# Grouped query attention on one core: one query product for all heads, spread by transfers within SBUF, and values of 32 columns

## The chip, the cores and the metric

The kernel runs on one core of one Trainium2 chip. Its five engines run their own instruction queues and meet through semaphores: TensorE (PE) multiplies matrices into PSUM, VectorE (DVE) and ScalarE (ACT) read PSUM and SBUF, GpSimd (POOL) does the indirect transfers and some elementwise work, and SyncE (SP) issues most transfers. The metric is the device time of one execution in microseconds, the median of several runs, without the profiler.

## The reference

The program is a two-layer block over x of 16 sequences, 256 tokens each, 128 features, all in float32. Layer 0 is half a mixture of experts, grouped query attention, half the same mixture again. Layer 1 is half a zone network, latent attention, half the zone network again. The part that is changed is layer 0's attention:

```
q = x @ Wq + bq                      # 16 heads of 8 columns
k = x @ Wk + bk                      # 4 key heads of 8 columns
v = x @ Wv + bv                      # 4 value heads of 8 columns
q = q.reshape(B, N, 4, 4, 8)         # key head g, query head j of the group, d
scores = einsum('bghnd,bhsd->bghns', q, k)
attn = softmax(scores / sqrt(8))
out  = einsum('bghns,bhsd->bghnd', attn, v) @ Wo + bo
```

Here x has been layer-normalised. Each key head g serves the four query heads 4g to 4g+3.

## The kernel before, in words

Tokens are split into eight blocks of 512 (two sequences each, `TB = 512`, `NB = 2`). The blocks stay in SBUF as `xs[0..7]` through the whole program. The stages follow one another: experts (`moe_first`), attention (`gqa`), experts (`moe_second`), zones, latent attention (`mla`), zones.

The attention keeps key head g in partition rows 32g to 32g+31, of which eight hold the head's columns, so that four products with 32 rows of contraction can stand in four row quarters of the PE array. The matrices are laid out for this on the host (`_layout`, helper `columns`): `w_q0` is four matrices of 128x128, one for each j, mostly zeros; `w_k0` and `w_v0` are 128x128 with the same gaps.

For each block, `gqa_rest` (L889) gives a list of small steps, `todo`: `head` (transposes the normalised block to `xnT`, L894; POOL adds the output bias to x, L896), `keys` (one product, L905, and an ACT evacuation, L906), `queries(j)` for four j (a product 128x512, L910, and an evacuation with scale and bias, by DVE for even j, L913, by ACT for odd j, L915) and `values` (four products 128x128, L922, and a DVE evacuation with bias, L925). The tiles `kT`, `qT` and `v` have three buffers each. The row after the eight columns of each head carries a one in the keys and in the values, and in the queries the negated largest score.

`gqa` (L1072) runs over sequences, n = 0 to 19, in four overlapping steps: the sequence `new` gets its scores and their maxima (`score` L937, the DVE reduction L976); `last` sends its maxima into the spare rows of `qT` (`send_largest`: PE transposes L1011, a DVE copy L1013, four transfers from SP, L1016); `old` gets the transposed scores with the maxima in them (`again` L949) and ACT's exponential (L980); `older` is multiplied with the values (`weigh` L1026), divided by its sums (`over_sums` L1043 to L1048) and finally turned and projected (`turned` L1058, `project` L1068). Each n has eight units, k = 0 to 7. One unit is eight products `score` or `again`, two reductions and two exponentials (`units` L959). After each unit PE gets a few `pieces`, among them one step of the next block's `todo`: in the block's first sequence (b = 0) after units 5, 6 and 7, in its second (b = 1) after units 0, 5, 6 and 7 (L1112). In n = 0 and 1 there is no `old`, and `wide_units` (L982, reductions L992) is used; n = 14 and 15 have no next block, so no `todo` steps.

Between these steps stand pieces of other work (`ahead`, from `beside_attention` L836): the shared expert of the first mixture (L634, L642, L643, L652) in n = 0 and later, and the routing of the second mixture from n = 8 on. At the start of each block, `gqa_pre(t + 1)` adds the experts' results to the next block on DVE (L788, eight operations) and normalises it.

The scores and exponents have three PSUM banks each, and all other products share two, the tag `pb` (L63). A scheduler orders the instructions of each engine when the program is built; each engine then runs its own list in that order.

POOL's list at the turn from experts to attention is: the two bias additions L896, then the gathers `y<-moe_y` (L772, eight for each block) that fetch the experts' results. The first of these waits until the last experts' tile has been written to DRAM (L745).

Of the kernel before, what the change touches and what calls it, by code (L numbers as in the profile page):

```python
# [12 lines left out]
F32 = mybir.dt.float32  # L13
I32 = mybir.dt.int32
U32 = mybir.dt.uint32
AF = mybir.ActivationFunctionType
ALU = mybir.AluOpType
# [3 lines left out]
P = 128  # L21
D = 128
SEQ = 256
TB = 512
NB = TB // SEQ
NTT = TB // P
NST = SEQ // P
# [10 lines left out]
H0, G0, J0, HD0 = 16, 4, 4, 8  # L38
SCALE0 = HD0 ** 0.5
# [11 lines left out]
def macaron_kernel(ctx: ExitStack, tc: tile.TileContext, a: dict, out: bass.AP):  # L51
# [3 lines left out]
    nc = tc.nc  # L55
# [4 lines left out]
    cpool = ctx.enter_context(tc.tile_pool(name="const", bufs=1))  # L60
# [4 lines left out]
    psum, stage = {}, {}  # L65
# [5 lines left out]
    def pb(shape):  # L71
        return psb.tile(shape, F32, tag="pb", name="pb")


    def load(name, shape=None, start=0):
        src = a[name]
        t = cpool.tile(list(shape or src.shape), F32, tag=name, name=name)
        nc.sync.dma_start(t[start : start + src.shape[0]], src)
        return t

    def load_rows(name):
        src = a[name]
        t = cpool.tile([P, src.shape[0]], F32, tag=name, name=name)
        nc.sync.dma_start(t, src.partition_broadcast(P))
        return t
# [54 lines left out]
    tile_no = counting("tile_no", NSLOT, 1)  # L140
    w_q0, w_k0, w_v0, w_o0 = load("w_q0"), load("w_k0"), load("w_v0"), load("w_o0")
    b_q0, b_k0 = load("b_q0"), load("b_k0")
    b_qs = cpool.tile([P, J0], F32, tag="b_qs", name="b_qs")
    nc.gpsimd.tensor_scalar(b_qs, b_q0, 1.0 / SCALE0, None, ALU.mult)
    b_v0, b_o0 = load_rows("b_v0"), load_rows("b_o0")
    w_r1, b_r1, w_r2, b_r2 = load("w_r1"), load("b_r1"), load("w_r2"), load_rows("b_r2")
# [143 lines left out]
    def turn_block(xn):  # L290
        xnT = pre.tile([P, TB], F32, name="xnT")
        transpose4(xn, xnT)
        return xnT
# [53 lines left out]
    for c in range(2):  # L347
        s = cpool.tile([P, 4, AHEAD + NPT, E0], F32, tag=f"sums{c}", name=f"sums{c}")
# [537 lines left out]
    def gqa_pre(t):  # L886
        return gqa_rest(t, normalised(t))

    def gqa_rest(t, xn):  # L889

        q = dict(t=t)

        def head():
            q["xnT"] = turn_block(xn)  # L894
            xt = xs[t]
            nc.gpsimd.tensor_tensor(  # L896
                xt, xt, b_o0.unsqueeze(1).to_broadcast([P, NTT, D]), ALU.add
            )

        def keys():  # L900
            pool = stage["pool"]
            q["kt"] = pool.tile([P, TB], F32, name="kT", bufs=3)
            q["qa"] = pool.tile([P, J0, TB], F32, name="qT", bufs=3)
            pk = pb([P, TB])
            nc.tensor.matmul(pk, w_k0, q["xnT"], start=True, stop=True)  # L905
            nc.scalar.activation(q["kt"], pk, AF.Identity, bias=b_k0)  # L906

        def queries(j):
            pq = pb([P, TB])
            nc.tensor.matmul(pq, w_q0[:, j, :], q["xnT"], start=True, stop=True)  # L910
            dst, bias = q["qa"][:, j, :], b_qs[:, j : j + 1]
            if j % 2 == 0:
                nc.vector.tensor_scalar(dst, pq, 1.0 / SCALE0, bias, ALU.mult, ALU.add)  # L913
            else:
                nc.scalar.activation(dst, pq, AF.Identity, bias=bias, scale=1.0 / SCALE0)  # L915

        def values():

            q["v"] = stage["pool"].tile([P, NTT, P], F32, name="v", bufs=3)
            pv = pb([P, NTT, P])  # L920
            for i in range(NTT):
                nc.tensor.matmul(  # L922
                    pv[:, i, :], q["xnT"][:, ts(i, P)], w_v0, start=True, stop=True
                )
            nc.vector.tensor_tensor(  # L925
                q["v"], pv, b_v0.unsqueeze(1).to_broadcast([P, NTT, P]), ALU.add
            )

        q["todo"] = [head, keys] + [partial(queries, j) for j in range(J0)] + [values]
        return q  # L930

# [84 lines left out]
    def weigh(q, half, s):  # L1018

        b, v, pT = q["b"], q["v"], q["pT", half]  # L1020
        if s == 0:
            q["po"] = pb([P, 2, SEQ])
            if half == 0:
                q["ov"] = stage["pool"].tile([P, J0, SEQ], F32, name="ov", bufs=2)
        for g in range(G0):
            nc.tensor.matmul(  # L1026
                q["po"][ts(g, 32)],
                v[:, b * NST + s, ts(g, 32)],
                pT[:, s, g, :],
                start=(s == 0),  # L1030
                stop=(s == NST - 1),
            )
        if s == NST - 1:
            copy = nc.vector.tensor_copy if half == 0 else nc.scalar.copy
            copy(q["ov"][:, ts(half, 2), :], q["po"])
# [36 lines left out]
    def gqa(block, after):  # L1072

        seqs = []
        rest = None

        def at(n):
            return seqs[n] if 0 <= n < len(seqs) else None

        ahead = after()  # L1080
        for f in block["todo"]:
            f()
        for n in range(2 * NBLK + 4):
            t, b = divmod(n, NB)
            if t < NBLK:
                if b == 0:
                    if rest is not None:
                        block = rest
                    rest = None
                    if t + 1 < NBLK:  # L1090
                        with tc.issue_after(reduced["last"].ins) if n else ExitStack():
                            rest = gqa_pre(t + 1)
                seqs.append(dict(block, b=b))
            elif n == 2 * NBLK:
                rest = None

            new, last, old, older, oldest = at(n), at(n - 1), at(n - 2), at(n - 3), at(n - 4)
            if n >= 2 * NBLK:
                new = None
            pieces = [[] for _ in range(8)]  # L1100
            if last is not None and n <= 2 * NBLK:
                pieces[0].append(partial(send_largest, last))
            if oldest is not None:
                pieces[0].append(partial(turned, oldest))
                pieces[2].append(partial(project, oldest))
            if older is not None:
                for k in range(4):
                    pieces[1 + k].append(partial(weigh, older, k // 2, k % 2))
                pieces[6].append(partial(over_sums, older, 0))
                pieces[7].append(partial(over_sums, older, 1))  # L1110
            if rest is not None and t < NBLK:
                for k in (5, 6, 7) if b == 0 else (0, 5, 6, 7):  # L1112
                    pieces[k].append(rest["todo"].pop(0))
            for k in range(8):
                half, s, g = k // 4, k // 2 % 2, k % 2
                if new is not None and old is not None:
                    units(half, s, 2 * g, new, old)
                elif g == 0:
                    wide_units(half, s, new, old)
                for f in pieces[k]:  # L1120
                    f()
                with tc.issue_after(reduced["last"].ins):
                    for f in ahead.get((n, k), ()):
                        f()
# [383 lines left out]
    with in_pools(1, dict(score=3, exp=3)):  # L1508
        gqa(ready, partial(beside_attention, *moes))
# [13 lines left out]
def _layout(inputs):  # L1523
# [3 lines left out]
    g = {k: np.asarray(v) for k, v in inputs.items()}  # L1527
    f32 = np.float32
    a = {"x": g["L0_attn_x"].reshape(-1, D)}
# [23 lines left out]
    def columns(w, heads):  # L1553

        out = np.zeros((w.shape[0], G0, 32), f32)
        out[:, :, :HD0] = w.reshape(w.shape[0], -1, HD0)[:, heads]
        return out.reshape(w.shape[0], P)

    each = np.arange(G0)
    wq, bq = g["L0_attn_Wq"], g["L0_attn_bq"][None]  # L1560
    a["w_q0"] = np.stack([columns(wq, each * J0 + j) for j in range(J0)], axis=1)
    a["b_q0"] = np.concatenate([columns(bq, each * J0 + j) for j in range(J0)]).T
    a["w_k0"] = columns(g["L0_attn_Wk"], each)
    b_k = columns(g["L0_attn_bk"][None], each).reshape(G0, 32)
    b_k[:, HD0] = 1.0
    a["b_k0"] = b_k.reshape(P, 1)
    a["w_v0"] = columns(g["L0_attn_Wv"], each)
    b_v = columns(g["L0_attn_bv"][None], each).reshape(G0, 32)
    b_v[:, HD0] = 1.0
    a["b_v0"] = b_v.reshape(P)  # L1570

    a["w_o0"] = g["L0_attn_Wo"]
    a["b_o0"] = g["L0_attn_bo"]
# [53 lines left out]
```

## Time and profile before

| | us |
|---|---|
| median of 3 runs without the profiler | 1584.16 (1581.67 to 1584.79) |
| the profiled execution's own time | 1779.86 |
| its span, which all views below are of | 1778.0 |
| experts, from the start of the span | 0 to 300 |
| attention with wide units (n = 0, 1), roughly | 300 to 380 |
| attention, n = 2 to 15 | 380 to 705 |
| attention's last weights, without new scores | 705 to 780 |
| second experts | 780 to 1040 |
| zones, latent attention, zones | 1040 to 1778 |

The profiled execution is 12% longer than the runs. In the views, PE is TensorE's products, PEld its weight loads, and a float32 product appears as two records[...]. "xcount" is the number of records, "mean ns of one" the mean length of a record, and the part after the bar is the idle time of that engine just before such records, with what ended it. The chain of waits is the chain of work that ended last, followed back from the end. Lines such as L910 are lines of the kernel before; the change moves later lines by some 20.

### The profile page before, as it was taken

The numbers are of one execution on the slowest core, as the hardware profiler recorded it, in microseconds if no ns is written. First come the engines' busy times: TensorE is split into PE (matmuls) and PEld (weight loads), VectorE is DVE, ScalarE is ACT, GpSimd is POOL, SyncE is SP. The second block draws the span as 40 slices with busy tenths as digits, with TensorE's granted clock in tenths as the row PEclk, the third lists the DMA queues.
The fourth block names the chain that finished last, engine by engine and source line by source line (L and its number), as shares of the span: only waits on it lengthen the run. The fifth ranks groups of instructions, "written<-read, shape, count | busy, mean of one in ns | idle before, by whom it ended". The sixth has DMA issues, their size and how long they took to land.

```text
span 1778.0 us, 26376 instructions
## 1 busy us (share of the span) xinstructions
PE 1489.0 (84%) x9010; PEld 963.9 (54%) x9010; DVE 956.0 (54%) x3132; ACT 572.5 (32%) x968; POOL 273.8 (15%) x330
## 2 busy tenths in 40 slices
PE   5556849799999798779565849999999999999998
PEld 3345636354444355236454627888644444458887
DVE  5434426466788586326334626554556666665432
ACT  2113313124455354414222303333222323224333
POOL 4441241211000302130242060000000000000000
PEclk9678959888999798799787879999999999999999
DMA  4316845000000000105565512444000000024442
GB/s 122 113 39 175 213 102 140 20 13 13 2 2 2 24 2 20 30 24 166 146 169 140 154 46 72 142 142 143 2 2 2 1 2 2 2 72 154 154 154 83
DMA packets 107541, 133.61 MB, mean 75 GB/s; under 512 B 13328, under 2 KB 78864, under 8 KB 107408
## 3 DMA queue, kind: packets, MB, share of 16 engines
q1 hardware_dynamic: 74192, 103.07, 19.4%
q0 software_dynamic: 8192, 16.79, 3.3%
q10 hardware_dynamic: 25024, 12.06, 2.3%
q8 instruction: 72, 1.18, 0.3%
q14 instruction: 61, 0.50, 0.1%
HBM read 104.62 MB, written 26.74 MB: 74 GB/s over the span
## 4 chain that ended last, share of the span: by engine, by line
PE 65%; DVE 8%; another core or an unknown queue 5%; issue 4%; ACT 1%; SPq 0%; DMA 0%; DVEq 0%; ACTq 0%
PE pb L1206 9%; PE pa L1192 9%; PE score L937 5%; PE pb L1026 4%; PE pa L709 4%; PE score L1325 4%; PE pb L1391 3%; PE exp L949 3%; PE exp L1364 3%; PE pb L634 2%; PE exp L1374 2%; PE pb L910 2%; PE pa L731 1%; DVE rs L1399 1%
## 5 line engine op out<-in xcount | busy, mean ns | idle before, releaser
L709 PE MATMUL pa<-moe_xT,moe_we 128*128 128x256 f32 x552 | 156.5, 417 | 53.4 <-issue 47.3
L937 PE MATMUL score<-kT,qT 32*128 32x256 f32 x960 | 173.7, 439 | 20.4 <-DVE nm L976 20.2
L976 DVE TENSOR_REDUCE nm<-score 128x2 f32<-128x512 f32 x224 | 144.9, 685 | 75.2 <-PE exp L949 57.2
L1192 PE MATMUL pa<-xnT,zone_m 128*128 128x256 f32 x768 | 185.3, 381 | 0.0
L1206 PE MATMUL pb<-zh,zone_m 128*128 128x256 f32 x768 | 179.8, 381 | 0.0
L949 PE MATMUL exp<-qT,kT 32*128 32x512 f32 x480 | 179.4, 703 | 0.0
L980 ACT ACTIVATE pT<-exp 128x512 f32<-128x512 f32 x224 | 123.4, 595 | 157.3 <-PE exp L949 146.2
L772 POOL DMA_INDIRECT y<-moe_y,moe_index x128 | 121.3, 947 | 323.9 <-DMA moe_y<-moe_yt 150.7
L937 PEld LDWEIGHTS score<-kT,qT 32*128 32x128 f32 x960 | 103.4, 201 | 121.9 <-DVE nm L976 61.8
L519 POOL DMA_INDIRECT moe_rows<-pair_xn,moe_slot x128 | 123.8, 967 | 288.5 <-DVE moe_w L537 102.0
L1200 ACT ACTIVATE zh<-pa 128x1024 f32<-128x1024 f32 x96 | 98.0, 1023 | 192.0 <-PE pa L1192 191.8
L1206 PEld LDWEIGHTS pb<-zh,zone_m 128*128 128x128 f32 x768 | 144.8, 190 | 19.4
L1192 PEld LDWEIGHTS pa<-xnT,zone_m 128*128 128x128 f32 x768 | 142.2, 190 | 18.1 <-issue 0.4
L709 PEld LDWEIGHTS pa<-moe_xT,moe_we 128*128 128x128 f32 x552 | 100.9, 200 | 74.5 <-issue 49.0
L1332 DVE TENSOR_REDUCE nm<-score 128x4 f32<-128x1024 f32 x64 | 77.1, 1205 | 62.9 <-PE score L1325 62.9
L1378 ACT ACTIVATE pT<-exp 128x1024 f32<-128x1024 f32 x64 | 62.2, 1021 | 147.5 <-PE exp L1374 147.5
L731 PE MATMUL pa<-moe_we,moe_h 128*128 128x128 f32 x368 | 62.9, 292 | 53.8 <-DVE h L718 28.5
L711 ACT ACTIVATE moe_sg<-pa 128x256 f32<-128x256 f32 x92 | 35.3, 383 | 187.8 <-PE pa L709 111.8
L731 PEld LDWEIGHTS pa<-moe_we,moe_h 128*128 128x128 f32 x368 | 57.1, 203 | 65.6 <-issue 56.2
L1026 PE MATMUL pb<-pT,v 128*32 128x512 f32 x512 | 76.2, 657 | 15.9 <-ACT oT L1062 15.9
L699 DVE COPY moe_xT<-pb 128x256 f32<-128x256 f32 x92 | 38.9, 424 | 88.1 <-remote 47.2
L1325 PE MATMUL score<-kt,qa 64*128 64x256 f32 x512 | 76.6, 409 | 11.2 <-DVE qa L1307 10.2
(265 smaller groups left out, 2301.6 us busy)
## 6 DMA issues: line engine op xcount, KB each, us to landing
zone_m<-in_w_z_dram SPq DMA_DIRECT2D x96, 512.0 KB
moe_we<-in_w_ex_dram SPq DMA_DIRECT2D x92, 312.0 KB
moe_xg<-moe_rows SPq DMA_DIRECT2D x92, 128.0 KB
moe_y<-moe_yt ACTq DMA_DIRECT2D x92, 128.0 KB
moe_rows<-zero_rows SPq DMA_DIRECT2D x32, 128.0 KB
x<-in_x_dram SPq DMA_DIRECT2D x8, 256.0 KB
moe_rows<-pair_xn,moe_slot POOLq DMA_INDIRECT x128
y<-moe_y,moe_index POOLq DMA_INDIRECT x128
```

What stands on the lines that cost most here:

```text
L519: nc.gpsimd.indirect_dma_start(out=part["views"].pop()[:, :], out_offset=bass.IndirectOffsetOnAxis(ap=slot[:, k, i : i + 1], axis=0), in_= ...
L709: nc.tensor.matmul(dst, q["w"][:, cols], q["xT"], start=True, stop=True)
L731: nc.tensor.matmul(py[:, i], q["h0"][:, ts(i, P)], q["w"][:, at : at + P], start=True, stop=False)
L772: nc.gpsimd.indirect_dma_start(out=y[:, k, i, :], out_offset=None, in_=part["y"][:, :], in_offset=bass.IndirectOffsetOnAxis(ap=part["index ...
L937: nc.tensor.matmul(sc[:, j % 2, :], qa[rows, j, ts(b * NST + st, P)], kt[rows, ts(b, SEQ)], start=True, stop=True,)
L949: nc.tensor.matmul(sc, kt[rows, ts(b * NST + s, P)], qa[rows, ts(half, 2), ts(b, SEQ)], start=True, stop=True,)
L976: reduced["last"] = nc.vector.tensor_reduce(new["nm"][:, s, g1 + c, ts(half, 2)], scores[c], AX.X, ALU.max, negate=True)
L980: nc.scalar.activation(old["pT", half][:, s, g0 + c, :], exps[c], AF.Exp)
L1026: nc.tensor.matmul(q["po"][ts(g, 32)], v[:, b * NST + s, ts(g, 32)], pT[:, s, g, :], start=(s == 0), stop=(s == NST - 1),)
L1192: nc.tensor.matmul(ps[:, f, :], mats[b * K1 + k][:, 0, ts(f, P)], xnT[:, ts(b, SEQ)], start=True, stop=True,)
L1206: nc.tensor.matmul(pz, mats[b * K1 + k][:, 1, ts(f, P)], h[:, f, :], start=(f == 0), stop=(f == NF1 - 1),)
L1325: nc.tensor.matmul(sc[:, p, slot, :], qa[rows, 2 * half + slot, ts(b * NST + st, P)], kt[rows, ts(b, SEQ)], start=True, stop=True,)
```

## The change

- `w_q0` becomes one 128x128 matrix whose output rows are (d, g, j), d the column in the head. `queries` makes one product 128x512, ACT evacuates it to a new tile `qn`, and eight transfers issued from SP, one for each d, move 16 rows of `qn` (2 KB each) to the rows 32g + d of `qT`, one row of each quarter, all four j behind one another.
- `qT` and `v` become three kept buffers each (`gqa_bufs`), made and cleared when blocks 0, 1 and 2 are prepared: `qT` of 128x2048 by DVE for block 0 and by POOL for blocks 1 and 2, `v` of 128x512 by POOL, and a column of ones in `v` by POOL.
- `w_v0` has 32 columns instead of 128 (no gaps). The four products are 128x32, and the DVE evacuation writes 128x128 elements into the eight columns of each group of 32 of `v`.
- The `todo` list is `head, queries, keys, values`. In the first sequence three steps are placed after units 5, 6 and 7 as before; in the second only `values`, after unit 0. Nothing of it stands after units 5, 6 and 7 of the second sequence.

In the order that is built, the first block's part of each engine's list reads as follows. PE: the query product, the key product, the four value products, four products of the shared expert (L634), then the scores of two units. DVE: the copy to `xnT`, the clearing of `qT`, the evacuation of `v`, then the reductions. POOL: the two bias additions, eight gathers, the clearing of `v`, one gather, the ones of `v`, seven gathers, the clearing of the other four buffers. SP: eight transfers for block 0, eight for block 1, then the first `send_largest`. The order of the other stages is the same but for a few neighbouring instructions.

```diff
-    b_qs = cpool.tile([P, J0], F32, tag="b_qs", name="b_qs")
+    b_qs = cpool.tile([P, 1], F32, tag="b_qs", name="b_qs")
...
+        def queries():
+
+            if t < 3:
+                gqa_bufs.append(
+                    (
+                        stage["pool"].tile([P, J0, TB], F32, name=f"qT{t}", bufs=1),
+                        stage["pool"].tile([P, NTT, G0, 32], F32, name=f"v{t}", bufs=1),
+                    )
+                )
+                qa, v = gqa_bufs[t]
+                (nc.vector if t == 0 else nc.gpsimd).memset(qa, 0.0)
+                nc.gpsimd.memset(v, 0.0)
+                nc.gpsimd.memset(v[:, :, :, HD0 : HD0 + 1], 1.0)
+            q["qa"], q["v"] = gqa_bufs[t % 3]
+            qn = stage["pool"].tile([P, TB], F32, name="qn", bufs=1)
+            pq = pb([P, TB])
+            nc.tensor.matmul(pq, w_q0, q["xnT"], start=True, stop=True)
+            nc.scalar.activation(qn, pq, AF.Identity, bias=b_qs, scale=1.0 / SCALE0)
+            for d in range(HD0):
+                nc.sync.dma_start(q["qa"][d::32], qn[ts(d, H0)])
...
-        def queries(j):
-            pq = pb([P, TB])
-            nc.tensor.matmul(pq, w_q0[:, j, :], q["xnT"], start=True, stop=True)
-            dst, bias = q["qa"][:, j, :], b_qs[:, j : j + 1]
-            if j % 2 == 0:
-                nc.vector.tensor_scalar(dst, pq, 1.0 / SCALE0, bias, ALU.mult, ALU.add)
-            else:
-                nc.scalar.activation(dst, pq, AF.Identity, bias=bias, scale=1.0 / SCALE0)
-
         def values():

-            q["v"] = stage["pool"].tile([P, NTT, P], F32, name="v", bufs=3)
-            pv = pb([P, NTT, P])
+            pv = pb([P, NTT, G0, HD0])
...
-                q["v"], pv, b_v0.unsqueeze(1).to_broadcast([P, NTT, P]), ALU.add
+                q["v"][:, :, :, 0:HD0],
+                pv,
...
-        q["todo"] = [head, keys] + [partial(queries, j) for j in range(J0)] + [values]
+        q["todo"] = [head, queries, keys, values]
...
-                for k in (5, 6, 7) if b == 0 else (0, 5, 6, 7):
+                for k in (5, 6, 7) if b == 0 else (0,):
```

More of the change, by code (lines that the diff above doesn't have):

```diff
@@ L898, in head @@
             )
+        def queries():
[17 more added lines that the diff above has]
+                nc.sync.dma_start(q["qa"][d::32], qn[ts(d, H0)])
         def keys():
-            pool = stage["pool"]
-            q["kt"] = pool.tile([P, TB], F32, name="kT", bufs=3)
-            q["qa"] = pool.tile([P, J0, TB], F32, name="qT", bufs=3)
+            q["kt"] = stage["pool"].tile([P, TB], F32, name="kT", bufs=3)
             pk = pb([P, TB])
@@ L906, in keys @@
             nc.scalar.activation(q["kt"], pk, AF.Identity, bias=b_k0)
-        def queries(j):
-            pq = pb([P, TB])
-            nc.tensor.matmul(pq, w_q0[:, j, :], q["xnT"], start=True, stop=True)
-            dst, bias = q["qa"][:, j, :], b_qs[:, j : j + 1]
-            if j % 2 == 0:
-                nc.vector.tensor_scalar(dst, pq, 1.0 / SCALE0, bias, ALU.mult, ALU.add)
-            else:
-                nc.scalar.activation(dst, pq, AF.Identity, bias=bias, scale=1.0 / SCALE0)
         def values():
-            q["v"] = stage["pool"].tile([P, NTT, P], F32, name="v", bufs=3)
-            pv = pb([P, NTT, P])
+            pv = pb([P, NTT, G0, HD0])
             for i in range(NTT):
                 nc.tensor.matmul(
-                    pv[:, i, :], q["xnT"][:, ts(i, P)], w_v0, start=True, stop=True
+                    pv[:, i].rearrange("p g d -> p (g d)"),
+                    q["xnT"][:, ts(i, P)],
+                    w_v0,
+                    start=True,
+                    stop=True,
                 )
             nc.vector.tensor_tensor(
-                q["v"], pv, b_v0.unsqueeze(1).to_broadcast([P, NTT, P]), ALU.add
+                q["v"][:, :, :, 0:HD0],
+                pv,
+                b_v0.rearrange("p (g d) -> p g d", g=G0)
+                .unsqueeze(1)
+                .to_broadcast([P, NTT, G0, HD0]),
+                ALU.add,
             )
-        q["todo"] = [head, keys] + [partial(queries, j) for j in range(J0)] + [values]
+        q["todo"] = [head, queries, keys, values]
         return q
+    gqa_bufs = []
     def score(q, sc, st, g, j):
@@ L1027, in weigh @@
                 q["po"][ts(g, 32)],
-                v[:, b * NST + s, ts(g, 32)],
+                v[:, b * NST + s, g],
                 pT[:, s, g, :],
@@ L1559, in _layout @@
     each = np.arange(G0)
-    wq, bq = g["L0_attn_Wq"], g["L0_attn_bq"][None]
-    a["w_q0"] = np.stack([columns(wq, each * J0 + j) for j in range(J0)], axis=1)
-    a["b_q0"] = np.concatenate([columns(bq, each * J0 + j) for j in range(J0)]).T
+    wq = g["L0_attn_Wq"].reshape(D, G0, J0, HD0).transpose(0, 3, 1, 2)
+    a["w_q0"] = wq.reshape(D, P)
+    a["b_q0"] = g["L0_attn_bq"].reshape(G0, J0, HD0).transpose(2, 0, 1).reshape(P, 1)
     a["w_k0"] = columns(g["L0_attn_Wk"], each)
@@ L1566, in _layout @@
     a["b_k0"] = b_k.reshape(P, 1)
[L1567 to L1570, printed above, removed]
+    a["w_v0"] = g["L0_attn_Wv"]
+    a["b_v0"] = g["L0_attn_bv"]
     a["w_o0"] = g["L0_attn_Wo"]
```

## The prediction

> **What bounds the kernel now.** I read the page first, then busy time by stretches, then the chain of waits and the timeline inside the attention.
>
> ```profile
> PE 1489.0 (84%) x9010; PEld 963.9 (54%) x9010; DVE 956.0 (54%) x3132; ACT 572.5 (32%) x968; POOL 273.8 (15%) x330
> PE 65%; DVE 8%; another core or an unknown queue 5%; issue 4%; ACT 1%; SPq 0%; DMA 0%; DVEq 0%; ACTq 0%
> ```
>
> PE holds 65% of the chain. The change touches only 300 to 705 us:
>
> ```profile
> 300.00:380.00 80.00, 67.13 (x347) 36.44 (x348) 42.74 (x95) 14.06 (x24) 17.36 (x19) 0.91 0.07 18
> 380.00:705.00 325.00, 299.74 (x2150) 152.79 (x2150) 237.10 (x635) 150.44 (x281) 40.43 (x41) 0.89 0.03 9
> ```
>
> The columns after the length are the busy time of PE, PEld, DVE, ACT and POOL. PE is busy 92% of the second stretch, DVE 73%. The operations that go or shrink, in the list of groups for 300 to 780:
>
> ```profile
> L910 PE MATMUL pb<-xnT,w_q 128*128 128x512 f32 x64 | 35.1, 636 | 0.0
> L922 PE MATMUL pb<-w_v,xnT 128*128 128x128 f32 x64 | 8.6, 277 | 0.0
> L925 DVE TENSOR_TENSOR v<-pb,b_v 128x512 f32<-128x512 f32 x8 | 5.5, 684 | 4.9 <-remote 3.0 <-PE pb L922 1.9
> ```
>
> Two records make a product, so a query product is about 1 us of PE (in the chain of waits, two records take 0.86 or 1.06). All 32 would be 28 to 34 us and 24 go. That alone says -23 us. But a busy PE is not a bounding PE, so I looked at what starts the next unit. First three units of block 6's second sequence (n = 13, 5, 6 and 7), then a unit of the last block, which has no query step:
>
> ```profile
> 653.95 0.48 PE L937 MATMUL score<-kT,qT 32*128 32x256 f32 x1
> 655.02 1.12 PE L910 MATMUL pb<-xnT,w_q 128*128 128x512 f32 x2
> 656.07 0.48 PE L937 MATMUL score<-kT,qT 32*128 32x256 f32 x1
> 658.59 0.48 PE L937 MATMUL score<-kT,qT 32*128 32x256 f32 x1
> 661.14 0.48 PE L937 MATMUL score<-kT,qT 32*128 32x256 f32 x1
> ```
>
> ```profile
> 674.49 0.48 PE L937 MATMUL score<-kT,qT 32*128 32x256 f32 x1
> 675.78 1.29 DVE L976 TENSOR_REDUCE nm<-score 128x2 f32<-128x512 f32 x2 [0.78 <-PE exp L949]
> 676.53 0.18 PEld L937 LDWEIGHTS score<-kT,qT 32*128 32x128 f32 x1 [0.88 <-DVE nm L976]
> ```
>
> Unit 5 with its query product takes 2.12 us (653.95 to 656.07), without it 2.04 (674.49 to 676.53). PE then waits for a reduction: of three score banks a unit uses two, and the next unit cannot fill its second before DVE has emptied one. The product sits almost wholly in that wait.
>
> [...] a score record takes 374 ns as a rule and up to 792 after waits. [...] Issue is seen here (four L1016 in 2.49 us); landing is not shown. [...] ACT and DVE stop together near POOL's gathers (DVE until 324.38, ACT until 328.69)[...].
>
> **The change part by part.**
>
> *Blocks 2 to 7, units 5, 6, 7 of the second sequence: two query products and the value step go.* Unit 5: 2.12 - 2.04 = 0.08. Unit 6: 656.07 to 658.59 is 2.52 with transposes and query; in the last sequence, without the query, 699.96 to 701.61 is 1.65, but unit 7's second score bank then starts 0.31 later than in a filled unit. Gain 0.87 - 0.31 = 0.56. Unit 7: 2.55 now. Its two reductions (1.29), reciprocal (0.25) and multiply (0.29) make 1.83 on DVE, with a handover some 2.0. Gain 0.55. Together 1.2. A check on DVE's side: unit 7's reductions end 7.14 after unit 5 starts (653.95 to 661.09), in the last sequence 6.5 (697.85 to 704.4), gain 0.65; then the value evacuation (0.68), which stands ahead of the next block's normalisation where PE waits for DVE (1.90 us at 427), leaves that place: 1.3. I take 1.3.
>
> *Unit 0 of the second sequence:* a query product (0.86 to 1.06) is replaced by the value products. Do 32 columns cost less than 128? The nearest row is L450, 128x9 after the same weight load: sixteen records take 1.90 to 2.03 us, 0.12 each; L922's eight take 0.89, 0.11 each. Weight loads set both, so nothing is gained by narrower values. Gain about 0.1. The smaller evacuation (0.29 as L1048, same elements) is on DVE where it waits for PE: nothing. First sequence: the one query step is as long as the step it displaces: nothing. ACT loses one evacuation of 0.69 a block; ACT waits for PE (146 us before L980), so nothing. DVE loses two of 0.75; in units with filler it waits 0.2 to 0.8 for PE, so nothing beyond the above.
>
> So 1.4 a block; low 0.5 (DVE's work at the turn of the block takes the rest), high 3 x 0.96 + 0.1 = 3.0 (PE alone). Six blocks: 8.4, from 3 to 18.
>
> *Block 1, in n = 0 and 1:* three products of 0.9 on PE, and the chain there also holds a query evacuation (0.70) and the value evacuation (0.68). PE waits more for ACT and DVE here. I take 2.5, from 0 to 4.1.
>
> *Transfers, blocks 1 to 7:* eight issues at 2.49 / 4 = 0.62 are 5 us of SP, from unit 6 of the first sequence; `send_largest` of unit 0 is queued behind them. Its rows are needed one sequence (some 20 us) later, the queries two or three units short of that. Nothing; if the cover went, 5 us a block.
>
> *Block 0, the added wait.* The clearing of `qT` is 2 x 0.91 = 1.8 on DVE (L1278, 128x1024, 0.91) while PE multiplies. The eight transfers: query product 302.7 to 303.7, evacuation to 304.5, issue until 309.5[...]. PE meanwhile has keys, values and shared expert, whose work stood after the first scores before. That would be hidden. But `v` is cleared by POOL behind eight gathers:
>
> ```profile
> 305.87 0.95 POOL L772 DMA_INDIRECT y<-moe_y,moe_index  x1 [11.87 <-DMA moe_y<-moe_yt]
> 317.13 0.94 POOL L772 DMA_INDIRECT y<-moe_y,moe_index  x1 [0.30 <-issue]
> L1278 POOL MEMSET rows<- x2: 957/957/957, 1257.7 to 1258.6; 128x1024 f32 x2
> ```
>
> They start at 305.87, one each 1.25 us: eight until 315.9, clearing 0.5, a ninth gather, the ones: 317.9. The value evacuation on DVE waits for this, all of DVE's reductions behind it, and PE, because the value sums hold one of two `pb` banks: the third product of the shared expert waits from about 308.7 until 318.3, 9.6 us, then starts on a cold clock (about 3 us more). Against that, 2.9 us of query products go. So +9.7 at most, if before had no wait there. But before stood still as well, from 315.07 for 13.64 us ("another core or an unknown queue"), and reached the next product, L652, at 329.34. By my count after reaches it at 328 to 330. So 0 to 1 in the profiled execution; without the profiler[...], up to +9.7. I take +5.
>
> *Start of the program:* smaller loads (256 to 64 KB, 64 to 16, 64 to 16), queued behind x: nothing, at most -1.
>
> **Sum:** -8.4 - 2.5 + 5 = -5.9. Against the profiled execution's own time, 1779.86, that is 1774 (1769 if its start costs nothing). The microseconds are set by PE and DVE durations, so I carry them over unscaled to the median: 1584.16 - 5.9 = 1578.3. I forecast 1578; by its bounds, start 0 to 9.7 and the loop from 8 to 14, its own range is 1570 to 1585.
>
> **The rivals.**
>
> *PE bounds all of it.* For: 92% busy, nearly all 32 query products in the chain of waits. Against: the fillerless unit at 674.49. 21 products at 0.96 and seven evacuations partly: -20, start -1: 1563.
>
> *The start eats the gain (slower).* The mechanism is `v`'s clearing behind POOL's gathers. For: the built order and the gathers' times. Against: before stands still at the same place. Price: 9.6 + 3 = 12.6 if the removed query products were themselves under waits, and block 1 gains nothing: -8.4 + 12.6 = +4: 1588. It decides from a start cost above the loop's gain, 8.4 to 11.
>
> *The products go but the time doesn't:* start and loop cancel, within 3 us of 1584.
>
> **How the numbers follow.** My forecast 0.55, PE bounds 0.2, slower start 0.15, no change 0.1. A measurement of this kernel can tell about 0.2% (3.2 us) from no change. Faster by more: most of the forecast's case (0.46), all of PE bounds: 0.66. Slower by more: 0.13 of the rival and 0.01: 0.14. Within: 0.20. The range reaches towards both rivals: 1565 to 1589.
>
> **What would show it.** Right: units 5 to 7 of second sequences begin with PE waiting for L976's successor; six blocks' period falls from 42.3 to 43.7 by about 1.4; the new value products still take 0.11 to 0.12 a record; DVE idles at its first value evacuation until about 318 on POOL. Wrong: a period falling by 3 (PE bounds), L652's successor reached well after 330 (the start costs more), or PE waiting for a transfer at a later block's first scores.

## The result, and the profile after

After takes 1596.45 us (median of 20 runs, 1587.27 to 1603.57), before 1585.39 in the same measurement: ratio 1.0055, with a 95% interval of 1.0035 to 1.0074. I had forecast 1578, faster. Groups of runs came in two kinds, a short one in which before takes about 1585 us (mean TensorE clock near 0.95) and a long one in which it takes about 1785 (near 0.90), so every kernel below is compared with before in its own group; the profile that the prediction read is of the long kind, the profile of after of the short.

The page of after, its busy times and its chain of waits:

```profile
PE 1459.4 (91%) x8962; PEld 956.7 (60%) x8962; DVE 946.4 (59%) x3117; ACT 567.4 (36%) x960; POOL 278.0 (17%) x338
PE 77%; DVE 11%; POOL 4%; issue 3%; DMA 2%; SPq 1%; ACT 1%; DVEq 0%; POOLq 0%
```

48 PE records are gone (24 query products), as the change says. "Another core or an unknown queue", 5% of the chain in the prediction's profile, is not in the list at all. The groups of after that answer to the query and value groups of before:

```profile
L916 PE MATMUL pb<-xnT,w_q 128*128 128x512 f32 x16 | 8.7, 626 | 0.0
L931 PE MATMUL pb<-w_v,xnT 128*128 128x32 f32 x64 | 8.5, 277 | 0.1
L938 DVE TENSOR_TENSOR v<-pb,b_v 128x128 f32<-128x128 f32 x8 | 2.3, 286 | 14.4 <-POOL v L911 11.8 <-PE pb L931 2.6
```

The last row holds the first finding: the shorter evacuation waited once for 11.8 us, for POOL.

To see where the time went, a profile of before of the short kind is needed. Its fourth profile (b2 below, span 1583.6) is one. Both spans are cut at the starts of the copies to `xnT` (L250), of the last score, of the attention's last projection (L1068, in after L1088) and of the last product of the second experts' shared part (L652):

| stretch, us | before (b2) | after | e4 (below) |
|---|---|---|---|
| start to block 0 | 218.4 | 219.1 | 217.7 |
| block 0 to block 1 | 23.60 | 37.26 | 25.97 |
| block 1 to 2 | 56.99 | 55.24 | 55.22 |
| 2 to 3 | 40.41 | 40.69 | 40.51 |
| 3 to 4 | 42.42 | 40.11 | 40.09 |
| 4 to 5 | 43.57 | 42.04 | 42.02 |
| 5 to 6 | 45.13 | 44.38 | 44.37 |
| 6 to 7 | 47.62 | 45.91 | 45.89 |
| 7 to the last score | 66.16 | 65.17 | 65.17 |
| to the last projection | 68.8 | 68.8 | 68.8 |
| second experts | 229.9 | 240.8 | 234.9 |
| the rest | 700.6 | 696.3 | 702.4 |

After against before: 13.7 lost in block 0, 8.8 gained from block 1 to the last score, 10.9 lost in the second experts. The rest, whose work is the same, gives 4.3 back; its length scatters from 692 to 702 over the fourteen profiles, also between two kernels that are the same in this stretch (e4 702.4, e5 696.4). With 0.7 at the start that is 12.2, the difference of the spans.

**Block 0.** Three lines of the timeline of after, from POOL, DVE and PE:

```profile
233.12 0.54 POOL L911 MEMSET v<- 128x512 f32 x1
233.69 0.29 DVE L938 TENSOR_TENSOR v<-pb,b_v 128x128 f32<-128x128 f32 x1 [11.76 <-POOL v L911]
234.04 2.08 PE L634 MATMUL pb<-moe_xnT,w_sg 128*128 128x512 f32 x2 [7.92 <-DVE v L938]
```

POOL clears `v` after eight gathers. DVE stands for 11.76 us at the evacuation, and PE for 7.92 us, because the values hold one of its two `pb` banks. Then two records take 2.08 us that otherwise take 1.10: the granted clock is 0.50 from 230 to 240 us and 0.55 until 250. In b2 there is no stop here. The stretch in b2, then in after (start and end, length, busy time of PE, PEld, DVE, ACT and POOL with the number of records, clock, and the share and GB/s of the DMA engines):

```profile
218.40:242.00 23.60, 23.39 (x120) 12.14 (x120) 13.73 (x24) 4.82 (x8) 14.70 (x16) 1.00 0.18 53
219.10:256.36 37.26, 27.80 (x114) 14.19 (x114) 13.53 (x23) 4.13 (x7) 20.45 (x24) 0.73 0.16 44
```

**Second experts.** The chain of waits in order of time, after:

```profile
671.75 2.51 PE pb L652 x20
674.28 0.37 SPq L684
...
675.57 2.48 DMA moe_xg<-moe_rows
678.09 0.45 PE pb L697 x2
...
679.05 2.93 PE pa L709 x6
```

and before (b2), from the same product on:

```profile
666.21 2.51 PE pb L652 x20
...
669.01 0.86 DVE x L661 x3
...
670.26 1.56 PE pa L709 x6
```

In after SP issues the first expert's weights (L684) only when the last product of the attention's shared expert has ended, 15.6 us after the last projection. The rows' transfer (L689), which SP issues next, then lies in the chain: PE waits 3.84 us for it and its next six records take 2.93 us instead of 1.56. In b2 SP issues the load 6.0 us after the projection (653.1), and PE goes on without such a wait:

```profile
659.12 0.37 SPq L684 DMA_DIRECT2D moe_we<-in_w_ex_dram  x1
```

No instruction of this stage was changed. What was changed is where things lie. The second experts' tiles reuse the attention's SBUF. By the tile sizes in the kernel (KB in each partition), their first weight tile begins 36 KB above the attention's first tile, behind the nine zone matrices of 4 KB. Before, 36 KB of `kT`, `qT` and `v` came first and the weights fell into the first buffer of `pT` (L634 to L652 keep the shared expert's values there). In after the buffers of blocks 1 and 2 are made later, `pT` begins at 18 KB, and the weights fall into its second buffer, which the last shared expert uses.

The price of this in the trace is 4.8 us: from the last projection to the second expert's first product (L709) b2 takes 19.4 us, after 24.3. In e4 and e5 below, whose layout is mended, it is that of b2 to 0.01 us. The rest of the 10.9 us arises later in the stage, and e4 is 5.0 us above b2 there too, which I can't explain.

### The profile page after: what moved, and what is told of

It is laid out like the page before. It is cut to its first block, busy times and chain, and to the rows that moved or that the text cites. A ratio compares the mean times of both kernels' runs of the same rounds, so it can differ in the third digit from the quotient of the medians.

```text
span 1595.8 us, 26364 instructions
## 1 busy us (share of the span) xinstructions
PE 1459.4 (91%) x8962; PEld 956.7 (60%) x8962; DVE 946.4 (59%) x3117; ACT 567.4 (36%) x960; POOL 278.0 (17%) x338
## 3 DMA queue, kind: packets, MB, share of 16 engines
q8 instruction: 72, 1.18, 0.3%
## 4 chain that ended last, share of the span: by engine, by line
PE 77%; DVE 11%; POOL 4%; issue 3%; DMA 2%; SPq 1%; ACT 1%; DVEq 0%; POOLq 0%
PE pb L1226 11%; PE pa L1212 10%; PE score L957 6%; PE pa L709 6%; PE pb L1046 4%; PE score L1345 4%; POOL y L772 4%; PE pb L1411 4%; PE exp L969 4%; PE exp L1384 3%; PE pb L634 3%; PE exp L1394 2%; PE pa L731 2%; PE pa L736 2%; PE pa L634 1%
## 5 line engine op out<-in xcount | busy, mean ns | idle before, releaser
L957 PE MATMUL score<-kT,qT 32*128 32x256 f32 x960 | 179.2, 439 | 10.0 <-DVE nm L996 9.4
L969 PE MATMUL exp<-qT,kT 32*128 32x512 f32 x480 | 186.2, 694 | 0.0
L957 PEld LDWEIGHTS score<-kT,qT 32*128 32x128 f32 x960 | 107.0, 201 | 102.6 <-DVE nm L996 51.7
L519 POOL DMA_INDIRECT moe_rows<-pair_xn,moe_slot x128 | 123.2, 963 | 229.9 <-DVE moe_w L537 95.8
L709 PE MATMUL pa<-moe_xT,moe_we 128*128 128x256 f32 x552 | 155.7, 415 | 5.8 <-issue 3.1
L709 PEld LDWEIGHTS pa<-moe_xT,moe_we 128*128 128x128 f32 x552 | 100.5, 199 | 26.0 <-issue 4.8
L1345 PE MATMUL score<-kt,qa 64*128 64x256 f32 x512 | 77.1, 412 | 11.2 <-DVE qa L1327 10.2
L731 PEld LDWEIGHTS pa<-moe_we,moe_h 128*128 128x128 f32 x368 | 58.3, 206 | 47.4 <-issue 38.1
L1345 PEld LDWEIGHTS score<-kt,qa 64*128 64x128 f32 x512 | 44.9, 189 | 57.1 <-issue 23.5
```

Of the source, the lines that this page charges most:

```text
L519: nc.gpsimd.indirect_dma_start(out=part["views"].pop()[:, :], out_offset=bass.IndirectOffsetOnAxis(ap=slot[:, k, i : i + 1], axis=0), in_= ...
L709: nc.tensor.matmul(dst, q["w"][:, cols], q["xT"], start=True, stop=True)
L731: nc.tensor.matmul(py[:, i], q["h0"][:, ts(i, P)], q["w"][:, at : at + P], start=True, stop=False)
L957: nc.tensor.matmul(sc[:, j % 2, :], qa[rows, j, ts(b * NST + st, P)], kt[rows, ts(b, SEQ)], start=True, stop=True,)
L969: nc.tensor.matmul(sc, kt[rows, ts(b * NST + s, P)], qa[rows, ts(half, 2), ts(b, SEQ)], start=True, stop=True,)
L1345: nc.tensor.matmul(sc[:, p, slot, :], qa[rows, 2 * half + slot, ts(b * NST + st, P)], kt[rows, ts(b, SEQ)], start=True, stop=True,)
```

## The experiments

All ratios are to before in the same group, with 95% intervals.

**b0, before again** (no edit).

> The kernel before, unchanged, for a second profile of it: the first one was 12% longer than its runs. Both theories expect about 1585 us. If the stop of 13.6 us at the start of the attention (another core or an unknown queue) belongs to the kernel, it is here again, and the start of block 0 costs before as much as after; if it came with that one profiled execution, PE goes from the key product to the first shared-expert result without such a stop, and the start of before is about 8 to 11 us shorter than that of after.

1782.67 us, and again 5% "another core or an unknown queue" in the chain. So the profile of the prediction was no accident of one execution. Block 0 takes 38.1 and 39.2 us in these two profiles of before. The stops are not before's own, either: all eight profiles of the long kind, of whatever kernel, have 4 to 11% of them in the chain, and none of the six of the short kind has any.

**e1, block 0's `v` cleared by DVE.**

```diff
-                nc.gpsimd.memset(v, 0.0)
-                nc.gpsimd.memset(v[:, :, :, HD0 : HD0 + 1], 1.0)
+                (nc.vector if t == 0 else nc.gpsimd).memset(v, 0.0)
+                (nc.vector if t == 0 else nc.gpsimd).memset(v[:, :, :, HD0 : HD0 + 1], 1.0)
```

> After, with one thing changed: block 0's v buffer and its ones are cleared by DVE instead of POOL, so that no clearing stands behind gathers. Theory A (the wait for POOL at block 0 is the whole loss): DVE's idle of 11.8 us before its first value evacuation and PE's of 7.9 us go, the cold clock behind them too; the time falls by 10 to 13 us against after, to about 1584, that is 1 to 5 us below before. Theory B (the wait replaces one that before has too, and the loss lies in the loop or in PE's clock): the time stays within 3 us of after, 1594 to 1597.

0.9988 (0.9973 to 1.0003). After was not in this group, so the step from after is not measured here. This group is of the long kind. In e1's trace block 0 takes 39.5 us, no less than before: an unexplained stop stands where the wait was. From block 1 to block 7 it takes 285.3 us against 296.9 and 299.2, so the loop's gain is there; 293.6 us of second experts against 287.1 and 286.4 take about half of it back. That was the first sign of the second cause.

**e2, the query half alone** (values as before; the tile of the sent maxima has two buffers).

> Only the query half of the change: one query product and eight transfers a block into kept buffers, but values with 128 columns in rotating buffers as before (to fit in SBUF, the tile for the sent maxima has two buffers instead of three). No clearing of v exists. Theory A: no wait at block 0, and the query half carries all the gain of the loop: 1578 to 1585 us, equal to e1 within 3. Theory B, with the loss in the query half: 1592 or more. If the transfers' landing or SP's issuing costs anything, it shows here as PE waiting at a later block's first scores.

0.9982 (0.9967 to 0.9998), no different from e1 within intervals of nearly 3 us: the narrow values bring nothing that these runs can tell. The second experts are long here too, with 294.4 us.

**e3, the value half alone.**

> Only the value half: 32-column products and a 128x128 evacuation into kept buffers cleared by POOL, with the four query products of before. Theory A: the wait at block 0 is there in full and nothing is gained elsewhere: 1592 to 1598 us, 8 to 12 above before. Theory B: within 3 us of before, 1583 to 1588.

1.0053 (1.0034 to 1.0072), as theory A said, but not for its reason. The wait itself is there:

```profile
318.08 0.29 DVE L934 TENSOR_TENSOR v<-pb,b_v 128x128 f32<-128x128 f32 x1 [8.66 <-POOL v L905]
```

Yet block 0 takes 39.1 us, as in before: in this kind of execution the wait lies beside a stop that is there without it. The loss lies elsewhere: in the second cause (the first rows, L689, were issued 15.6 us after the last projection, and the second experts take 291.3 us) and in 66.6 us from block 6 to 7 against 61.5 to 61.8 in before, which I can't explain. The number agreed, the reason did not: e3 proves nothing for A.

**a0, e5, e4: after, then its layout undone, then the wait taken away as well**, in one group. e5 is after with

```diff
-            if t < 3:
-                gqa_bufs.append(
-                    (
-                        stage["pool"].tile([P, J0, TB], F32, name=f"qT{t}", bufs=1),
...
+            if t == 0:
+                for u in range(3):
+                    gqa_bufs.append(
+                        (
+                            stage["pool"].tile([P, J0, TB], F32, name=f"qT{u}", bufs=1),
...
+            if t < 3:
```

and e4 is e5 with the edit of e1.

> After, unchanged, on the chip of this group. Its first measurement gave 8.7 to 11 us more than before. All theories: 0.35 to 0.75% above before.

> After (v of block 0 still cleared by POOL) with the layout of e4 alone. Theory C: 4 to 7 us below after, so 0.1 to 0.4% above before, with the start's wait of some 10 us still there. Rival D: equal to after.

> The kernel of e1 (block 0's v cleared by DVE) with one more thing changed: all three kept pairs qT and v are made when block 0 is prepared, so the tile pT, which the shared expert uses last, begins 20 KB later in SBUF, and the first weight tile of the second experts no longer lies in the pT buffer that is freed last. Theory C (layout): in e1 that first load, L684 on SP, was issued 16.0 us after the attention's last projection, before it was 6.4; here it is issued near 6, and the second experts, which were 7 us longer in e1 than before, lose 4 to 7 us: 0.4 to 0.7% below before. Rival D (the second experts were longer by chance, or by PE's clock): equal to e1, 0.1% below before.

a0: 1.0053 (1.0036 to 1.0071). e5: 1.0011 (0.9995 to 1.0027). e4: 0.9955 (0.9938 to 0.9973). On 1585 us the layout is worth (1.0053 - 1.0011) x 1585 = 6.7 us, the wait (1.0011 - 0.9955) x 1585 = 8.9 us, and what is left of the change gains 7.1. Each of these differences is uncertain by some 3 us. Theory A alone is wrong (the wait is not the whole loss), A and C together hold, D falls. In e4 and e5 the first weights are issued 6.0 us after the last projection. In the traces the same two edits show 4.8 us for the layout (above) and, for the wait, 36.17 us of block 0 in e5 against 25.97 in e4, that is 10.2.

e4 is the version that beats both kernels: 1579.53 us, in a group where before took 1584.72 and a0 1594.11.

**e6, before with the layout of after and nothing else.**

```diff
-            q["qa"] = pool.tile([P, J0, TB], F32, name="qT", bufs=3)
+            q["qa"] = pool.tile([P, J0, TB], F32, name=f"qT{t % 3}", bufs=1)
...
-            q["v"] = stage["pool"].tile([P, NTT, P], F32, name="v", bufs=3)
+            q["v"] = stage["pool"].tile([P, NTT, P], F32, name=f"v{t % 3}", bufs=1)
```

> The kernel before with the SBUF layout that the change makes, and nothing else: the three buffers of qT and of v get tags of their own, as in after, so that those of blocks 1 and 2 lie behind pT, and the second experts' first weight tile comes to lie in the pT buffer that the last shared expert uses. Theory C: 4 to 8 us above before, 0.3 to 0.5%, all of it after the attention. Rival D (the layout matters only together with the rest of the change, or not at all): equal to before.

1.0038 (1.0018 to 1.0057), 6.8 us on 1786. First a wait of SP's queue in e6 (total, times, longest), then a line of PE's timeline:

```profile
SPq L684 <- DVE pT L643: 76.9, 1, 76.9
```

```profile
820.70 0.69 PE L697 MATMUL pb<-ident,moe_xg 128*128 128x128 f32 x2 [3.44 <-DMA moe_xg<-moe_rows]
```

PE waits for the first rows, with not one instruction added or removed. The second experts take 293.3 us against 285.7 in before of the same group (b1, below). The layout alone does it, at the price that a0 and e5 gave in the short kind (6.7).

**e8, `pT` still higher**: e4 with `ov`, `on` and `oT` made first.

> The kernel of e4 with pT moved up another 12 KB (ov, on and oT are made first), so that none of the second experts' first five weight tiles lies in a pT buffer. Theory C: the first weights are issued when the routing's table is there, before the shared expert ends; one to three us below e4 if the weights are what the first expert waits for, equal to e4 if it waits for the rows, whose tile still lies in pT.

0.9958 (0.9941 to 0.9976), like e4 in its group. SP's timeline:

```profile
727.77 0.37 SPq L684 DMA_DIRECT2D moe_we<-in_w_ex_dram  x1
797.66 0.39 SPq L689 DMA_DIRECT2D moe_xg<-moe_rows  x1
```

The weights go out 70 us earlier, the rows, whose tile still lies in `pT`, 6.0 us after the last projection as in e4, and nothing is won. In e8, as in e4, PE waits for neither: its first product on the rows follows the shared expert's last without idle time.

```profile
807.08 0.38 PE L697 MATMUL pb<-ident,moe_xg 128*128 128x128 f32 x2
```

**e7, spare products**: e4 with two unread 128x512 products put back in each block's second sequence.

```diff
+        def spare():
+            nc.tensor.matmul(pb([P, TB]), w_q0, q["xnT"], start=True, stop=True)
...
-                for k in (5, 6, 7) if b == 0 else (0,):
+                for k in (5, 6, 7) if b == 0 else (0, 5, 6):
```

> The kernel of e4 with two products of 128x512 put back after units 5 and 6 of each block's second sequence, where before had query products; nothing reads them. It adds work and leaves none out. My prediction's account (they sit in PE's wait for the reductions): 14 products cost 0.3 to 0.6 us each block-pair, 3 to 6 us together. If PE bounds the loop: 14 times 0.96, 13 us.

0.9979 (0.9958 to 0.9999), 3.8 us above e4. Fourteen products of some 1 us cost a quarter of their time. Two blocks of e4 (4 to 5, 5 to 6) and of e7 with the same clock, 0.92; the columns are as above:

```profile
379.45:421.47 42.02, 40.21 (x310) 20.97 (x305) 32.87 (x94) 20.57 (x38) 1.26 (x1) 0.92 0.02 8
421.47:465.84 44.37, 43.15 (x318) 22.45 (x313) 35.31 (x104) 22.78 (x43) 1.27 (x1) 0.92 0.02 8
```

```profile
387.53:430.24 42.71, 40.96 (x314) 20.85 (x309) 32.83 (x94) 20.57 (x38) 1.27 (x1) 0.92 0.02 8
430.24:474.96 44.72, 43.55 (x322) 22.45 (x317) 35.31 (x104) 22.68 (x43) 1.26 (x1) 0.92 0.02 8
```

Four more records, 0.69 and 0.35 us longer. Over blocks 1 to 7 e7's trace is 9.1 us longer than e4's, but the clocks differ in the other stretches (3 to 4: 43.4 us at 0.92 against 40.1 at 1.00), and e7's profiled run is the slowest of its runs. Single units, which can be compared, come below. "PE bounds all of it" falls: it needed 1.9 a block.

**b1 and b2, before once more, for a profile of the short kind.**

> The kernel before, unchanged, for a profile at the clock of the runs (about 0.95), to set against the profile of after stage by stage. From block 0's xnT to block 1's after takes 37.2 us; with the wait removed (e4) 26.0. My account of the whole: before takes 25 to 28 there, about 1 us more than after in each later block, and issues the first weights of the second experts some 6 us after the attention's last projection, after 15.6.

> The kernel before once more, for a profile at the clock of the runs (0.95), if this chip gives it. If the loop gained in after what I predicted (11 us from block 0's end on), block 1 to block 7 takes about 279 us here against 268 in after; if it gained only the 5 us that e4 leaves, about 271 to 273. Block 0 to block 1: 26 to 29 us, against 37.2 in after and 26.0 in e4.

b1 came out at 1788.12 us, of the long kind, and serves only as the partner of e6. b2 came out at 1585.39 and is the table's first column. Block 1 to block 7 takes 276.1 us in it against 268.4 in after. Block 0 to 1 takes 23.6, less than the 25 to 29 us that I expected.

## Why the prediction was wrong, point by point

- **Blocks 2 to 7, -8.4: right in mechanism and nearly in size.** From block 2 to the last score after is 7.0 us shorter (+0.3, -2.3, -1.5, -0.8, -1.7, -1.0). Much of the scatter goes with the granted clock: the block that did not fall had 0.97 in b2 and 0.89 in after, the one that fell most 0.96 and 1.00. In the last four the clock was the same, and they fell by 1.2 on average. The starts of single units in PE's timeline show the gain more cleanly (a unit is four products `score` and two `again`; products of 32 rows do stand side by side: in b2 sixteen such records of 256 columns are through in 1.08 us, 231.14 to 232.22, 0.07 each, where L1192's of 128 rows and as many columns take 0.24, 185.3 us for 768). For n = 5, each unit with the pieces after it:

| us | unit 0 | unit 5 | unit 6 | unit 7 | unit 0 of n = 6 | sum |
|---|---|---|---|---|---|---|
| before (b2) | 1.65 | 2.13 | 2.52 | 2.55 | 1.60 | 10.45 |
| after | 1.61 | 0.97 | 2.71 | 1.95 | 1.97 | 9.21 |
| e7 | 1.61 | 2.13 | 2.52 | 1.66 | 2.04 | 9.96 |

  Two query products and the value products left units 5 to 7, some 3 us of PE, and 1.2 came back; the two products that e7 puts back cost 0.75 together. In the second sequences of the five other blocks the same sum falls by about 1.2, too. So the prediction's 1.2 for these units (taken as 1.3, with 0.1 for unit 0) stands. Its split doesn't: it has 0.08 for unit 5, because it took 676.53 for the end of the unfilled unit. The next unit starts at 675.46, in its first free score bank, and 676.53 is that unit's second half. The unit without a product ends a whole product sooner, and the wait for the reductions follows in the next units.
- **Block 1, -2.5:** -1.75.
- **Narrow values, nothing on PE:** right. L931 takes 277 ns a record, as L922 did. The eight weight loads of block 0's values take 0.97 us in both (from 308.20 in the prediction's profile, from 222.28 in after), the records of the products behind them 1.16 and 1.08. The evacuation takes 286 ns, as estimated. e2 against e1 shows no gain, either.
- **Transfers of blocks 1 to 7, nothing:** right. No wait for one shows in after at a later block's scores.
- **Block 0, +5: this step failed.** In the prediction's words, "before stood still as well", so "0 to 1 in the profiled execution" and without the profiler "up to +9.7. I take +5." The stop of 13.6 us that I let stand against the wait is absent in the short kind of execution, the kind that I forecast, where before crosses the place in 23.6 us. The profiler isn't what makes it: whole groups of runs took 1785 us without it. The first product L652 tells the two kinds apart. Counted from block 0's copy to `xnT`, it starts after 27.7 to 28.6 us in all eight profiles of the long kind, with the wait (e3, 27.8) or without, so there "0 to 1" was right. In the short kind it starts after 15.6 us in b2 and 29.3 in after. My count for after, "328 to 330", is 26.5 to 28.5 from the copy (301.5), so the path of after was nearly right and that of before was not. The wait was therefore paid in full: 10.2 us in the traces of e5 and e4, 8.9 in their runs. The price of the slower rival, 9.6 + 3, was close, and I gave it 15%. The 3, for a slow clock after the wait, was an estimate. The prediction's profile has a case of it: after its stop, from the first L652 to the next unit's scores, PE takes 6.16 us (329.34 to 335.50, clock 0.57), the same records in b2 3.85 (234.01 to 237.86, clock 1.00). PE waited 7.92 us and not 9.6, because the evacuation waits for the clearing alone, not for the ones behind the ninth gather.

  A further 2.4 us (25.97 - 23.60) is left in e4, though three query products are gone there. PE is idle for 3.3 us of this stretch in e4 and for 0.2 in b2, and from 230 to 240 us the clock is 0.83 in e4 and 1.00 in b2. The first scores account for 0.87 of the idle time: they wait for the eight transfers, issued until 225.5.

```profile
228.14 0.48 PE L959 MATMUL score<-kT,qT 32*128 32x256 f32 x2 [0.87 <-DMA qT<-qn]
```

  I had called those hidden. Most of the other idle time is waits for ACT (0.69 twice) and DVE (0.50 and 0.35). So block 0 is +13.7 where the sum had +5.
- **Second experts, no term at all: the second failure.** I had compared the order of the instructions, found the other stages unchanged, and took that for "nothing". The order was the same; the memory was not. The sum lacked 4.8 us by the traces and 6.7 (a0 against e5) or 6.8 (e6) by the runs.
- **Put together** from the traces: -8.8 + 13.7 + 4.8 = +9.7, where the runs show 8.4 (1.0053) to 8.7 (1.0055) and the two profiles, with scatter in the unchanged stages, 12.2. My sum was -5.9. The loop missed by 2, block 0 by 9, the second experts by 5.

What stays open: what makes the two kinds of execution, and what the stops of the long kind are ("another core or an unknown queue"). It is not mainly TensorE's clock: PE is busy for 1489.0 us in the prediction's profile and for 1461.3 in b2, 28 us less, while the spans differ by 194. Each group of experiments ran on one chip; two chips gave the short kind, two others the long. The table of queues has the same 72 packets, 1.18 MB, of kind "instruction" (q8) for before in both kinds. That doesn't show how long each took, so it neither makes instruction transfers the cause nor rules them out. And since the step from after to e1 was not run in the long kind, what the wait costs there is known from the traces alone.

## What to carry to other kernels

A wait that a change adds may not be set off against a stop in the profile that no view explains: another execution may not have the stop, while the wait stays. So clear a kept buffer on an engine whose list is short at that moment, not behind a list of gathers. When tiles are kept, renamed or made at another time, look at which buffers of the next stage fall on which of this one, and who uses those last: the same instructions in the same order lost 5 to 7 us to it here, and making the kept tiles earlier mended it. Of work removed from a busy engine, count what starts the next piece: here 21 products of 1.09 us (64 records in 34.8 us in b2), 23 us, were worth 8.8.

## What the runs showed of the hardware that I had not expected

- A wait of 3.84 us before the second experts was followed by a slow clock: PE's next six records took 2.93 us instead of 1.56, at 0.50. In a0 and e6, after waits of 3.81 and 3.44 us here, they took 2.93 us as well; in before, b2, e4, e5 and e8, which have no such wait here, they took 1.56. So a wait of this length cost nearly 1.4 us more than itself. The slow clock also came without one: from 300 to 308 us of after it was 0.50, with PE busy throughout, and the longest wait in the 8 us before was 0.72 us. After the 7.92 us of block 0 the clock was 0.50 to 0.55 for some 16 us.
- Eight transfers within SBUF, 16 rows of 2 KB each (e4): 4.74 us to issue on SP's queue (0.59 each), and the first reader started 2.6 us after the last issue (228.14 - 225.49).
